# A four-layer cross-attention and FFN kernel on one core: router rows normalised tile by tile, first queries tile by tile, layer 1's conversions a gap earlier

## The chip, the cores and the metric

The kernel runs on one core of one Trainium2 chip. The metric is device microseconds of one execution; before the change the median of three executions is 1113.09 us (1112.28 to 1113.81). Engines are named as the profile names them: PE multiplies and transposes, DVE does vector work, ACT does activations and scaled copies, POOL does small vector work here and issues the indirect DMAs (gathers and scatters), SP issues the plain DMAs. Each engine runs its own instructions in the order in which they stand in its program; waits between engines are semaphores.

## What is computed

The input x is 2048 rows (tokens) of 256 values, in 8 batches of 256 rows. Four layers follow each other, and each adds a cross-attention over 77 context rows and then an FFN to x, both read from a normalised copy of x:

```python
x = x + jnp.tanh(g_xattn[1]) * _L1_xattn_ref(_layernorm(x), ctx, ctx, ...)   # one head
x = x + jnp.tanh(g_ffn[1])   * _L1_ffn_ref(_layernorm(x), W1, b1, W2, b2)    # rows quantised to 8 bits, ternary weights, 256 -> 1024 -> 256
x = x + jnp.tanh(g_xattn[2]) * _L2_xattn_ref(_layernorm(x), ctx, ctx, mask, 64, ...)  # 16 heads, the best 64 of 77 scores kept
x = x + jnp.tanh(g_ffn[2])   * _L2_ffn_ref(_layernorm(x), router_w, w1, w2)  # 8 experts, each row goes to its best 2, capacity 640
```

In layer 2's FFN the logits are `x_flat @ router_w.T` of the normalised rows; a row's place in its expert's buffer is a running count over all rows before it. Layers 0 and 3 are of the same build and are not touched.

## The kernel before

**Groups and tiles.** x stays on the chip in four groups `X[0]` to `X[3]` of 512 rows, each of `GT` = 4 tiles of 128 rows. Layer 0 is done for all groups first (to about 224 us of the span). Layer 1 is `cross1(g)` (attention of a group) and `ffns1(g)` (FFN of a group). Group 0 passes through both, and group 1 through `cross1`, before anything of layer 2 starts; the other groups are worked on between the tiles of layer 2.

**Layer 2's selection** is `select(n0, n1)` (L1398), a loop over the 16 tiles, run in two halves, tiles 0 to 7 and 8 to 15. `distances` makes a tile's scores (`sc`, L1052) from the queries of its group; ACT turns them into distances from the maximum (`pr`, L1072); then DVE drops the 13 lowest of 77 scores for 16 heads, with 2 x 16 MAX8 (L1410) and 2 x 16 MATCH_REPLACE8 (L1422). After every eighth of these it calls `gap()` (L1383): eight gaps a tile. In a gap the generators in `steps` are advanced, each in every second gap: `finish(n)` of the tiles before, `route`, `places`, `queries`, and `front`, which is layer 1's groups 1 to 3 (`groups1`). DVE's order is written out in this way by hand (`manual_schedule` with DVE alone); the order on PE, ACT, POOL and SP is chosen when the program is built, by a scheduler that goes by program order, by priority (`high_priority(AHEAD)`) and by when it takes an instruction to be ready.

**Queries.** `queries(g)` normalises a whole group (`normal_act`: bn_stats and bn_aggr on DVE, four small POOL operations, four ACT `xn` at L245, eight PE transposes L255, two ACT copies) and multiplies (`pq`, L1031, four matmuls of 128x512). `queries(0)` stands ahead of `select`, so tile 0 of the selection waits for all of group 0.

**End of a tile.** `finish(n)` (L1078): Abs and Exp on ACT (L1083, L1084), sums on DVE (`sm`, L1088), a product on POOL (L1090), transposes `pta` (L1096), copies `aT`, `po` (L1102), `oT2`, `py` (L1110, L1112), and, six of its steps after the start, the DVE operation at L1115 that adds the tile's result to x. At the last tile of a group it appends `route(g)`.

**Router.** `route(g)` (L1121) normalises the whole group with `normal_act`, writes it to DRAM (`xbuf`, one DMA of 512 KB for each half that needs it, six in all), three steps later multiplies 4 x 2 times with the router's weights (`pl`, L1141), a step later starts the softmax (`m`, L1148, `pb`, L1151) and a step later takes the best two experts. After groups 1 and 3 follows `places(h)`: it counts, by matmuls with triangular and block matrices (`ptc`, `pcn`, `pp`), each row's place, finds which expert each 128-row tile belongs to (`widx`), and inverts the places by 16 matmuls (`inv`, L1351, with `at_row`, L1348) into the rows of each tile (`tok`, L1364, `gate`, `row`).

**Experts.** `experts(h)` (L912) fetches a tile's rows from `xbuf` (`xg`, L919, needs `tok`) and its expert's weights of 2 MB (`wt`, L924, needs `widx`), transposes the rows (`ptm`), multiplies (`phm`, L948, then GELU `hT` L952, `pym`, L960), scales (`yo`, L965) and scatters into `ybuf` (L970). `experts(0)` has 16 tiles and runs beside the second half of the selection; `experts(1)` needs `places(1)`, has 22 and more, and runs beside layer 3.

**Layer 1's FFN.** `ffn1(n)` is one tile: quantised rows `xi`, transposes `ptx` (L664), `ph` (L672, L676) with GELU (`h`, L677); two steps later the row maximum `am2` (L681) and an ACT pass that scales and rounds (L686); at the next step `hi` (L688, DVE, to bf16), eight transposes `pth` (L691), a copy `hiT` (L693), `pyf` (L696); at the next step the add to x (L700). `ffns1` starts the tiles in pairs and advances a tile at every second call.

**PSUM.** Eight banks. Ahead of the selection a pool of eight is split into five for `cross1(0)` and `ffns1(0)` and three for the rest; it is closed, and then three (`psm`), two (`psc`, the scores) and three (`ps`) are opened.

Of the kernel before, what the change touches and what calls it, by code (L numbers as in the profile page):

```python
# [9 lines left out]
F32 = mybir.dt.float32  # L10
# [9 lines left out]
P = 128  # L20
D = 256
# [37 lines left out]
def flamingo_kernel(ctx: ExitStack, tc: tile.TileContext, io: dict):  # L59
# [597 lines left out]
    def ffn1(n, ps, f1w, xn, up, dn, rT):  # L657
# [29 lines left out]
        yield  # L687
# [11 lines left out]
        yield  # L699
        nc.vector.scalar_tensor_tensor(  # L700
# [3 lines left out]
    def ffns1(g, ps, f1w, act):  # L704

        for rows in normal1(g, ps, f1w, act):
            yield
            yield
        fs = {}
        at = 0  # L710
        while at == 0 or fs:
            if at % 4 < 2 and (n := at // 4 * 2 + at % 2) < GT:
                fs[n] = ffn1(g * GT + n, ps, f1w, *rows)
            for n in [n for n in fs if n % 2 == at % 2]:
                if next(fs[n], fs) is fs:
                    del fs[n]
            at += 1
            yield
# [90 lines left out]
    with tc.tile_pool(name="a1p", bufs=8, space=PSUM, side="right", reuse_waits="tile") as ps:  # L809
        chain, ps = Banks(ps, "chain", 5), Banks(ps, "beside", 3)  # L810
        for _ in cross1(0, chain, b1w, *kv1, False):
            pass
        for _ in ffns1(0, chain, b1w, False):
            pass
        for _ in cross1(1, ps, b1w, *kv1, False):
            pass

        nm = a2.tile([P, NB, SK], BF16, name="nm")
        nmf = nm.rearrange("p b k -> p (b k)")
        nc.vector.tensor_copy(nmf, mask_u8)
        some = a2.tile([P, NB], F32, name="some")
        nc.vector.tensor_reduce(some, nm, AX.X, ALU.max)
        nc.vector.tensor_scalar(nmf, nmf, 2.0**100, -(2.0**100), ALU.mult, ALU.add)
        onesb = a2.tile([P, P], BF16, name="onesb")
        nc.vector.memset(onesb, 1.0)
        bq4 = a2.tile([P, KC], F32, name="bq4")  # L830
        nc.vector.tensor_scalar(bq4, cols[:, C_WQB * KC : (C_WQB + 1) * KC], 0.25, None, ALU.mult)
        wob3 = rows3(a2, V_WOB, "wob")

        kT2 = a2.tile([P, KC, NB, 2, SK], F32, name="kT2")
        V2 = a2.tile([SK, NB, 8, 2, 2, 16], F32, name="V2")
        nc.gpsimd.memset(V2.rearrange("p b r q s d -> p (b r q s d)"), 0.0)

        for hb in range(2):  # L840
            for oc in range(KC):
                pk = ps.tile([P, 512], F32, name="pk", tag="ps")
                for kc in range(KC):
                    nc.tensor.matmul(
                        pk[:, :HB], wk2[:, kc, oc * P : (oc + 1) * P],
                        ctxT[:, kc, hb * HB : (hb + 1) * HB],
                        start=(kc == 0), stop=(kc == KC - 1),
                    )
                for q in range(2):
                    nc.vector.tensor_scalar(  # L850
                        kT2[:, oc, 4 * hb : 4 * hb + 4, q, :],
                        pk[:, :HB].rearrange("p (b k) -> p b k", k=SK),
                        col(C_WKB, oc), par[:, q : q + 1], ALU.add, ALU.mult,
                    )
            for b in range(4 * hb, 4 * hb + 4):
                pv = ps.tile([P, 512], F32, name="pv", tag="ps")
                for kc in range(KC):
                    nc.tensor.matmul(
                        pv[:SK, :D], ctxT[:, kc, b * SK : (b + 1) * SK], wv2[:, kc, :],
                        start=(kc == 0), stop=(kc == KC - 1),  # L860
                    )
                pvv = pv[:SK, :D].rearrange("p (r q d) -> p r q d", q=2, d=16)
                bvv = vrow(V_WVB, SK).rearrange("p (r q d) -> p r q d", q=2, d=16)
                for q in range(2):
                    nc.vector.tensor_add(V2[:, b, :, q, q, :], pvv[:, :, q, :], bvv[:, :, q, :])

# [45 lines left out]
    def experts(h, psm, f2w, widx, tok, gate, row, ahead=0):  # L912
# [91 lines left out]
    psm = ctx.enter_context(tc.tile_pool(name="f2p", bufs=3, space=PSUM, reuse_waits="tile"))  # L1004
    banks = ExitStack()
    psc = banks.enter_context(
        tc.tile_pool(name="a2s", bufs=1, space=PSUM, side="right", reuse_waits="tile")
    )
    ps = banks.enter_context(
        tc.tile_pool(name="a2p", bufs=3, space=PSUM, side="right", reuse_waits="tile")  # L1010
    )
# [11 lines left out]
    qs = {}  # L1023

# [53 lines left out]
    def finish(n, pr):  # L1078
# [28 lines left out]
        oT = a2w.tile([P, KC, P], F32, name="oT2")  # L1107
# [9 lines left out]
        )  # L1117
        if t == GT - 1:
            steps.append(route(g))

    def route(g):  # L1121

        gs = slice(g * GT, (g + 1) * GT)

# [3 lines left out]
        bank = ps if g else psm  # L1128
        xn, xT = normal_act(g, bank)
        for h in range(g // 2, 2):  # L1130
            r = g % 2 * GN + (h - g // 2) * HN
            nc.sync.dma_start(
                out=xbuf[h][r : r + GN, :].rearrange("(t p) d -> p t d", p=P), in_=xn
            )
        yield
        yield
        yield
        pl = bank.tile([P, GT, NE], F32, name="pl", tag="ps")
        for t in range(GT):
            for kc in range(KC):  # L1140
                nc.tensor.matmul(  # L1141
                    pl[:, t, :], xT[:, kc, t * P : (t + 1) * P], rtr[:, kc, :],
                    start=(kc == 0), stop=(kc == KC - 1),
                )
        yield
# [252 lines left out]
    def select(n0, n1):  # L1398
# [4 lines left out]
        for n in range(n0, n1):  # L1403
            pr = nxt
            ahead = distances(n + 1) if n + 1 < n1 else iter(())
            rows = [pr[:, j, c, :] for j in range(4) for c in range(4)]
            for r in range(2):
                m8 = a2w.tile([P, H, 8], F32, name=f"m8{r}")
                for i, row in enumerate(rows):
                    nc.vector.max(m8[:, i, :], row)  # L1410
                    if i == H - 1:
                        while n + 1 < n1 and (n + 1) // GT not in qs:
                            gap()
                        with tc.high_priority(AHEAD):
                            nxt = next(ahead, None)
                    if i % 8 == 7:
                        gap()
                if r == 1:

                    nc.vector.memset(m8[:, :, NDROP - 8 :], -BIG)  # L1420
                for i, row in enumerate(rows):
                    nc.vector.match_replace(row, m8[:, i, :], row, -BIG)  # L1422
                    if i % 8 == 7:
                        gap()
# [7 lines left out]
    ordered = {mybir.EngineType.DVE}  # L1432
    with tc.manual_schedule(engines=ordered):
        with tc.high_priority(AHEAD):
            for _ in queries(0):
                pass
        front = groups1(psm, kv1)
        steps.append(front)
        select(0, HT)
        last = steps.pop()  # L1440
        while steps:
            gap()
# [327 lines left out]
```

## Time and profile before

| what | value |
|---|---|
| median of three executions | 1113.09 us |
| the profiled execution | 1113.11 us |
| its span, first to last instruction | 1111.3 us |
| PE busy | 911.4 us (82%) |
| DVE busy | 645.9 us (58%) |
| ACT busy | 511.2 us (46%) |
| POOL busy | 307.6 us (28%) |

Times below are microseconds from the start of the span. In the timeline the selection's first MAX8 stands at 302.8, tile 7's add to x at 541.9, the first expert matmul at 597.3, the selection's last MATCH_REPLACE8 at 729.1, the add of tile 15 at 758.1, and the first matmul of `experts(1)` at 805.1. A busy share is an average over stages with different limits, so the stages between these marks are read one by one.

### The profile page before, as it was taken

Reading aid. Unit: us, or ns where it says so; the run is one execution under the profiler, and the core shown is the slowest. Engines: PE = TensorE matmul, PEld = TensorE weight load, DVE = VectorE, ACT = ScalarE, POOL = GpSimd, SP = SyncE. Lnnn points to the kernel's source line nnn. Section 1 sums busy time; section 2 is a strip of 40 time slices with the busy share of each in tenths; the row PEclk is TensorE's granted clock in tenths of the full one; section 3 lists DMA queues with packets and bytes.
Section 4 is the critical chain, followed back from the end, with each engine's and each line's share of the span. In section 5 each row is a group of like instructions: output and inputs, shape, how many; then the busy total and the mean of one; then the engine's idle time right before and its main releaser. Section 6 shows DMA issues by size and latency. Waiting matters only on the chain.

```text
span 1111.3 us, 16751 instructions
## 1 busy us (share of the span) xinstructions
PE 911.4 (82%) x5896; PEld 667.3 (60%) x5896; DVE 645.9 (58%) x2834; ACT 511.2 (46%) x1026; POOL 307.6 (28%) x333
## 2 busy tenths in 40 slices
PE   4678798848968688696877998899999969897895
PEld 2456565634525344463455776787999867696663
DVE  4767966656586976988676687732700023501663
ACT  3333444117356576575555566644222236422551
POOL 2342124010020210120104233243345445331531
PEclk9668989978965776865566999999999989998696
DMA  6200000003000000010106544365888964383001
GB/s 227 94 1 3 1 1 1 1 1 152 1 1 1 1 1 1 1 39 1 39 1 229 193 168 175 116 230 201 301 307 319 360 237 180 105 300 124 10 10 38
DMA packets 27179, 115.77 MB, mean 104 GB/s; under 512 B 4324, under 2 KB 16332, under 8 KB 21973
## 3 DMA queue, kind: packets, MB, share of 16 engines
q0 software_dynamic: 9504, 90.71, 22.3%
q1 hardware_dynamic: 17589, 23.96, 6.0%
q8 instruction: 48, 0.79, 0.3%
q14 instruction: 38, 0.31, 0.1%
HBM read 99.19 MB, written 15.47 MB: 103 GB/s over the span
## 4 chain that ended last, share of the span: by engine, by line
PE 40%; DVE 25%; ACT 12%; POOL 9%; issue 8%; DMA 6%; SPq 1%; POOLq 0%; ACTq 0%; DVEq 0%
DVE pr L1422 3%; PE phm L948 3%; PE pta L1096 3%; DVE m L1410 3%; PE pym L960 3%; DMA yg<-ybuf 3%; PE py L488 2%; DMA ybuf<-yo,row 2%; PE po L1102 2%; PE pta L473 2%; POOL pr L1090 2%; DVE sm L1088 2%; PE ph L672 2%; ACT pr L1072 1%; POOL ybuf L970 1%
## 5 line engine op out<-in xcount | busy, mean ns | idle before, releaser
L948 PE MATMUL phm<-xgT,wt 128*128 128x128 f32 x1216 | 152.5, 280 | 1.4 <-DMA wt<-in_w,widx 0.9
L948 PEld LDWEIGHTS phm<-xgT,wt 128*128 128x128 f32 x1216 | 147.0, 195 | 5.7 <-issue 2.6
L960 PE MATMUL pym<-wt,hT 128*128 128x256 f32 x608 | 146.2, 385 | 3.0 <-ACT hT L952 3.0
L960 PEld LDWEIGHTS pym<-wt,hT 128*128 128x128 f32 x608 | 112.1, 193 | 18.5 <-ACT hT L952 4.4
L1422 DVE MATCH_REPLACE8 pr<-m,pr 128x77 f32<-128x77 f32 x512 | 107.3, 224 | 0.0
L1090 POOL TENSOR_TENSOR pr<-pr,sm 128x1232 f32<-128x1232 f32 x16 | 36.0, 2249 | 179.9 <-DVE sm L1089 161.6
L952 ACT ACTIVATE hT<-phm 128x512 f32<-128x512 f32 x76 | 45.4, 597 | 81.1 <-PE phm L948 81.0
L1410 DVE MAX8 m<-pr 128x8 f32<-128x77 f32 x512 | 76.2, 222 | 0.0
L1096 PE MATMUL pta<-ident,pr 128*77 128x128 f32 x256 | 54.2, 352 | 18.4 <-POOL pr L1090 18.3
L1570 DVE TENSOR_TENSOR x<-x,yg 128x512 f32<-128x512 f32 x16 | 12.9, 808 | 94.7 <-DMA yg<-ybuf 94.7
L970 POOL DMA_INDIRECT ybuf<-yo,row x46 | 45.9, 997 | 74.0 <-ACT yo L965 58.3
L1098 ACT COPY aT<-pta 77x512 f32<-77x512 f32 x64 | 36.5, 588 | 61.8 <-PE pta L1096 61.8
L919 POOL DMA_INDIRECT xg<-xbuf,tok x38 | 38.6, 1015 | 93.9 <-PE ptm L935 42.2
L474 ACT COPY aT<-pta 77x512 f32<-77x512 f32 x64 | 35.4, 581 | 62.1 <-PE pta L473 62.1
L1072 ACT ACTIVATE pr<-sc,mx 128x77 f32<-128x77 f32 x256 | 58.8, 337 | 7.7 <-DVE mx L1067 7.7
L1052 PE MATMUL sc<-kT,qT 32*128 32x154 f32 x256 | 39.5, 406 | 26.9 <-ACT pr L1072 22.1
L456 POOL TENSOR_TENSOR pr<-pr,sm 128x1232 f32<-128x1232 f32 x16 | 36.8, 2299 | 89.1 <-DVE sm L455 45.6
L965 ACT ACTIVATE yo<-pym,gate 128x256 f32<-128x256 f32 x38 | 18.1, 476 | 93.4 <-PE pym L960 47.5
L924 POOL DMA_INDIRECT wt<-in_w,widx x38 | 37.2, 979 | 79.7 <-PE pym L960 71.0
L1096 PEld LDWEIGHTS pta<-ident,pr 128*77 128x77 f32 x256 | 37.8, 190 | 33.0 <-POOL pr L1090 21.3
L473 PE MATMUL pta<-ident,pr 128*77 128x128 f32 x256 | 44.7, 319 | 15.4 <-POOL pr L456 9.6
L473 PEld LDWEIGHTS pta<-ident,pr 128*77 128x77 f32 x256 | 33.4, 170 | 31.1 <-issue 12.9
(388 smaller groups left out, 1947.2 us busy)
## 6 DMA issues: line engine op xcount, KB each, us to landing
ybuf<-zero SPq DMA_DIRECT2D x8, 512.0 KB, 4.7
yg<-ybuf SPq DMA_DIRECT2D x16, 256.0 KB, 8.9
xbuf<-xn SPq DMA_DIRECT2D x6, 512.0 KB, 2.8
x<-in_x SPq DMA_DIRECT2D x4, 512.0 KB, 5.0
raw_f1w<-in_f1w SPq DMA_DIRECT2D x2, 1024.0 KB, 4.8
out<-x SPq DMA_DIRECT2D x8, 256.0 KB, 2.1
vec<-in_vec SPq DMA_DIRECT2D x1, 896.0 KB, 9.9
ybuf<-yo,row POOLq DMA_INDIRECT x46, 6.0
```

The costliest lines, as they stand in the source:

```text
L473: nc.tensor.transpose(pt[:SK, j, :], pn2[i][:, j, c, :], ident)
L919: nc.gpsimd.indirect_dma_start(out=xg[:, :], out_offset=None, in_=xbuf[h][:, :], in_offset=bass.IndirectOffsetOnAxis(ap=tok[:, m : m + 1], ...
L948: nc.tensor.matmul(ph[:, i, :], wt[:, kc * FF + fc * P : kc * FF + (fc + 1) * P], xgT[:, kc, :], start=(kc == 0), stop=(kc == KC - 1),)
L952: nc.scalar.activation(hT[:, NFC // 2 * fq : NFC // 2 * (fq + 1), :], ph, AF.Gelu)
L960: nc.tensor.matmul(py, hT[:, fc, :], wt[:, KC * FF + fc * D : KC * FF + (fc + 1) * D], start=(fc == 0), stop=(fc == NFC - 1),)
L970: nc.gpsimd.indirect_dma_start(out=dst[:, :], out_offset=bass.IndirectOffsetOnAxis(ap=row[:, m : m + 1], axis=0), in_=yo[:, :], in_offset= ...
L1052: nc.tensor.matmul(sc[:, jj, c * 2 * SK : (c + 1) * 2 * SK], qT[32 * j : 32 * j + 32, c, t * P : (t + 1) * P], kT2[32 * j : 32 * j + 32, c ...
L1072: nc.scalar.activation(pr[:, j0 + jj, c, :], sc[:, jj, c * SK : (c + 1) * SK], AF.Identity, bias=mx[:, jj, c : c + 1], scale=-1.0,)
L1090: nc.gpsimd.tensor_tensor(pr, pr, sm.unsqueeze(3).to_broadcast([P, 4, 4, SK]), ALU.mult)
L1096: nc.tensor.transpose(pt[:SK, j, :], pr[:, j, 2 * c + q, :], ident)
L1410: nc.vector.max(m8[:, i, :], row)
L1422: nc.vector.match_replace(row, m8[:, i, :], row, -BIG)
```

## The change

`route` no longer normalises a group. A new helper `normal_tile` does one tile, right behind the tile's add to x in `finish`; the tile's rows go to `xbuf` at once (128 KB each, 24 DMAs in place of six) and two steps later to the router's matmul, whose result is copied to an SBUF tile `logits`. At the last tile of a group `finish` goes straight on into `route`, which starts at the softmax. `queries(0)` is replaced by `queries0(t)`, one call for each tile of group 0: tile 0 ahead of the selection, tile 1 at its start, tiles 2 and 3 within tiles 0 and 1. Layer 2's keys (`pk`) are computed ahead of `cross1(1)`, its values (`pv`) behind it. The PSUM pools of the selection are opened ahead of layer 1's group 0, which now has three banks in place of five. In `ffns1` a tile whose ACT pass has just been issued is advanced at the next call and not at the one after it. The buffers of `oT2` (two, of 1 KB a partition) are shared with the new `xn_q0` and `xT_q0`.

```diff
@@ ffn1 @@
         nc.scalar.activation(h, h, AF.Identity, bias=magic, scale=up2)
-        yield
+        yield "soon"
         nc.vector.tensor_scalar(hi, h, MAGIC, 127.0, ALU.subtract, ALU.min)
...
         yield
+        yield
         nc.vector.scalar_tensor_tensor(
             X[g][:, t, :], py[:, :D], dn2, X[g][:, t, :], ALU.mult, ALU.add
         )
@@ ffns1 @@
         fs = {}
+        soon = set()
...
-            for n in [n for n in fs if n % 2 == at % 2]:
-                if next(fs[n], fs) is fs:
+            for n in [n for n in fs if n % 2 == at % 2 or n in soon]:
+                soon.discard(n)
+                step = next(fs[n], fs)
+                if step is fs:
                     del fs[n]
+                elif step:
+                    soon.add(n)
@@ layer 1's group 0 @@
-    with tc.tile_pool(name="a1p", bufs=8, space=PSUM, side="right", reuse_waits="tile") as ps:
-        chain, ps = Banks(ps, "chain", 5), Banks(ps, "beside", 3)
-        for _ in cross1(0, chain, b1w, *kv1, False):
-            pass
-        for _ in ffns1(0, chain, b1w, False):
-            pass
-        for _ in cross1(1, ps, b1w, *kv1, False):
-            pass
+    psm = ctx.enter_context(tc.tile_pool(name="f2p", bufs=3, space=PSUM, reuse_waits="tile"))
+    banks = ExitStack()
+    psc = banks.enter_context(
+        tc.tile_pool(name="a2s", bufs=1, space=PSUM, side="right", reuse_waits="tile")
+    )
+    ps = banks.enter_context(
+        tc.tile_pool(name="a2p", bufs=3, space=PSUM, side="right", reuse_waits="tile")
+    )
+    for _ in cross1(0, psm, b1w, *kv1, False):
+        pass
+    for _ in ffns1(0, psm, b1w, False):
+        pass
...
-        for hb in range(2):
-            for oc in range(KC):
-                pk = ...
-            for b in range(4 * hb, 4 * hb + 4):
-                pv = ...
+    for hb in range(2):
+        for oc in range(KC):
+            pk = ...
+    for _ in cross1(1, ps, b1w, *kv1, False):
+        pass
+    for b in range(NB):
+        pv = ...
@@ new helpers @@
+    def normal_tile(x, bank):
+        xn = a2w.tile([P, D], F32, name="xn_q0", tag="oT2")
+        xT = a2w.tile([P, KC, P], F32, name="xT_q0", tag="oT2")
...
+        nc.vector.bn_stats(st, x)
+        nc.vector.bn_aggr(mv, st)
+        rs = small.tile([P, 1], F32, name="q0_rs")
+        nc.gpsimd.tensor_scalar(rs, mv[:, 1:2], EPS, None, ALU.add)
+        nc.gpsimd.tensor_tensor(rs, rs, mhalf[:, :1], ALU.pow)
+        m = small.tile([P, 1], F32, name="q0_nm")
+        nc.gpsimd.tensor_tensor(m, mv[:, 0:1], rs, ALU.mult)
+        nc.gpsimd.tensor_scalar(m, m, -1.0, None, ALU.mult)
+        nc.scalar.activation(xn, x, AF.Identity, bias=m, scale=rs)
+        pt = bank()
+        for kc in range(KC):
+            nc.tensor.transpose(
+                pt[:, kc * P : (kc + 1) * P], xn[:, kc * P : (kc + 1) * P], ident
+            )
+        nc.scalar.copy(xT, pt.rearrange("p (c n) -> p c n", c=KC))
+        return xn, xT
+
+    def queries0(t):
...
+            _, xT = normal_tile(
+                X[0][:, t, :], lambda: ps.tile([P, KC * P], F32, name="ptq0", tag="ps")
+            )
+            pq = ps.tile([P, KC * P], F32, name="pqq0", tag="ps")
+        for oc in range(KC):
+            for kc in range(KC):
+                nc.tensor.matmul(
+                    pq[:, oc * P : (oc + 1) * P], wq2[:, kc, oc * P : (oc + 1) * P],
+                    xT[:, kc, :], start=(kc == 0), stop=(kc == KC - 1),
+                )
+            nc.scalar.activation(
+                qs[0][:, oc, rows], pq[:, oc * P : (oc + 1) * P], AF.Identity,
+                bias=bq4[:, oc : oc + 1], scale=0.25,
+            )
@@ finish @@
-        oT = a2w.tile([P, KC, P], F32, name="oT2")
+        oT = a2w.tile([P, KC, P], F32, name="oT2", tag="oT2")
...
+        xn, xT = normal_tile(X[g][:, t, :], lambda: ps.tile([P, KC * P], F32, name="ptr", tag="ps"))
+        for h in range(g // 2, 2):
+            r = g % 2 * GN + (h - g // 2) * HN + t * P
+            nc.sync.dma_start(out=xbuf[h][r : r + P, :], in_=xn)
+        yield
+        yield
+        if t == 0:
+            logits[g] = f2.tile([P, GT, NE], F32, name="logits", bufs=2)
+        pl = ps.tile([P, NE], F32, name="pl", tag="ps")
+        for kc in range(KC):
+            nc.tensor.matmul(
+                pl, xT[:, kc, :], rtr[:, kc, :], start=(kc == 0), stop=(kc == KC - 1)
+            )
+        nc.vector.tensor_copy(logits[g][:, t, :], pl)
         if t == GT - 1:
-            steps.append(route(g))
+            yield from route(g)
@@ route @@
+        pl = logits.pop(g)
-        bank = ps if g else psm
-        xn, xT = normal_act(g, bank)
-        for h in range(g // 2, 2):
-            r = g % 2 * GN + (h - g // 2) * HN
-            nc.sync.dma_start(
-                out=xbuf[h][r : r + GN, :].rearrange("(t p) d -> p t d", p=P), in_=xn
-            )
-        yield
-        yield
-        yield
-        pl = bank.tile([P, GT, NE], F32, name="pl", tag="ps")
-        for t in range(GT):
-            for kc in range(KC):
-                nc.tensor.matmul(
-                    pl[:, t, :], xT[:, kc, t * P : (t + 1) * P], rtr[:, kc, :],
-                    start=(kc == 0), stop=(kc == KC - 1),
-                )
-        yield
@@ select @@
+            if n == 0:
+                with tc.high_priority(AHEAD):
+                    queries0(1)
...
                     nc.vector.max(m8[:, i, :], row)
+                    if r == 1 and i == 0 and n + 2 < GT:
+                        with tc.high_priority(AHEAD):
+                            queries0(n + 2)
@@ ahead of the selection @@
+    with tc.high_priority(AHEAD):
+        queries0(0)
     with tc.manual_schedule(engines=ordered):
-        with tc.high_priority(AHEAD):
-            for _ in queries(0):
-                pass
```

## The prediction

> **What bounds the kernel now.** First the busy time of each engine in the stages between the marks of the table (windows view; busy us, instructions, granted PE clock, DMA share).
>
> ```profile
> core 0: us, PE busy (x) PEld busy (x) DVE busy (x) ACT busy (x) POOL busy (x), PEclk, DMA share, GB/s
> 240.00:303.00 63.00, 49.70 (x256) 29.05 (x256) 39.64 (x129) 27.90 (x47) 7.78 (x10) 0.86 0.17 67
> 303.00:525.00 222.00, 168.96 (x926) 96.45 (x925) 181.24 (x1048) 136.88 (x293) 36.46 (x42) 0.66 0.02 6
> 525.00:597.00 72.00, 52.77 (x272) 32.27 (x273) 55.20 (x334) 36.35 (x72) 9.32 (x10) 0.57 0.13 46
> 597.00:805.00 208.00, 190.84 (x1451) 160.97 (x1449) 122.34 (x769) 113.86 (x235) 71.29 (x69) 0.96 0.57 203
> ```
>
> Up to 303 PE sets the pace: its timeline is almost without gaps from 249 to 303, and DVE waits for it. From 303 to 597 DVE leads (181 of 222, 55 of 72), and what it loses are waits. From 597 to 805 PE leads: 191 of 208, its gaps of 0.5 us and more between 600 and 770 sum to about 15. From 805 on the order of the instructions does not change, so a shift at 805 is a shift of the end.
>
> Next what DVE waits for in 303 to 600 (line, releaser: total us, times, longest), then the two waits ahead of the selection and the one ahead of the router's softmax (timeline: start, us, instruction, idle before and releaser).
>
> ```profile
> DVE x L700 <- PE pyf L696: 16.6, 4, 9.7
> DVE am L681 <- ACT h L677: 6.7, 3, 4.2
> DVE m L1148 <- PE pl L1141: 5.0, 1, 5.0
> ```
>
> ```profile
> 297.85 0.80 DVE L1067 TENSOR_REDUCE mx<-sc 128x8 f32<-128x616 f32 x1 [7.06 <-PE sc L1060]
> 302.06 0.80 DVE L1067 TENSOR_REDUCE mx<-sc 128x8 f32<-128x616 f32 x1 [3.41 <-PE sc L1060]
> 554.10 0.19 DVE L1148 TENSOR_REDUCE m<-pl 128x4 f32<-128x32 f32 x1 [4.99 <-PE pl L1141]
> ```
>
> Last, the entrance to the experts: `tok` is written at 584.4 to 584.8, then POOL issues two gathers, and PE multiplies at 597.26.
>
> ```profile
> 585.09 1.23 POOL L919 DMA_INDIRECT xg<-xbuf,tok  x1 [39.99 <-PE pth L691]
> 586.62 0.96 POOL L924 DMA_INDIRECT wt<-in_w,widx  x1 [0.30 <-issue]
> ```
>
> Issue to landing is 4.7 us for xg and 9.4 for wt (medians), so the weights, issued second and needing only `widx` (ready some 9 us earlier), end the wait.
>
> **The change, part by part.** The sum is made against the profiled execution, 1113.11 us (span 1111.3 and 1.8 around it), which stands at the median, 1113.09.
>
> 1. *Start of the selection.* Ahead of the second MAX8 PE now does keys of layer 1's group 1 (4.5 us) and all of queries(0): transposes 0.6 + 0.6, matmuls 2.7 + 1.1, 5.1 in all. The keys stand elsewhere and two tiles' queries remain (2.6), which saves 7.0. Against it: `pk` (2 x 2.24) moves ahead of cross1(1), where only part of it is covered by gaps, cost about 1.7; three banks in place of five in layer 1's group 0, estimated 1. I take -4. Bounds: -8 (all saved, more overlap) and 0 (the banks eat it; `ffns1(0)` is 30 us of interleaved tiles, one wait of the size of the 4.2 us on L677 would do).
>
> 2. *First half of the selection.* "soon" puts `hi` and `pyf` a gap earlier and the add at L700 later, so its 16.6 us of waits should go. But in the new order `hi` follows the ACT pass directly: that pass (1.28) stands behind the distances (16 x .34, 1.82 left at that point), so DVE waits some 3 to 5 us in group 1 and about 1 in groups 2 and 3. Of 16.6 I keep 10 as waits of the new kind: -6.6; behind `hi` stand the MAX8 of the tile, so each of these waits is paid in full. The softmax's wait on `pl` falls from 5.0 to 1 (only one tile is left to multiply): -4. Added on DVE ahead of `tok`: 20 rows, 4.8 us by the rows they resemble (bn_stats .41, bn_aggr .18, copies .16 to .2): +5, paid, for DVE leads here. ACT gets four more table loads in this half at 1.28 each, 5.1 us, mostly in ACT's idle time (137 of 222 busy): +1.5. Sum -4. Bounds: -14 (all waits of L700 go and ACT hides its part) and +5 (they are only replaced).
>
> 3. *Weights ahead of rows.* In the new order both first weight gathers stand before `xg` and `tok` on POOL. Then `tok` to first matmul is xg alone: 0.3 + 1.2 + 4.7 + transposes, about 6.5 in place of 12.5: -6. Bounds -6 and 0 (if `widx` is late, or POOL's normalising rows, now queued around the gathers, hold them).
>
> 4. *Queries of groups 2 and 3 ahead of the experts.* 8 transposes and 4 matmuls (5.5 us), before at 610.9 behind the first expert matmuls, now stand ahead of them, in time in which PE waits: -5 (bounds -5.5 and 0).
>
> 5. *597 to 805, PE's stage.* In the new order the experts' tiles are further along: at tile 15's `py` 14.0 of 16 are done in place of 11.3, and all 16 stand ahead of the second `inv`. Work that covered the hand-over is so spent. From the end of the last `pl` (768.0) to the first possible matmul of experts(1) the chain is: counts and places on DVE to 793.3 (`xg` issued), 4.7 to landing, .5 of transposes: 30. PE has now only 17.4 us to do there (2.4 expert tiles at 7.25): idle 12.6, where today it is 0.46 (PE's timeline, idle before the first matmul of experts(1)):
>
> ```profile
> 804.21 0.42 PE L935 MATMUL ptm<-ident,xg 128*128 128x128 f32 x2
> 805.09 1.16 PE L948 MATMUL phm<-xgT,wt 128*128 128x128 f32 x8 [0.46 <-ACT xgT L937]
> ```
>
>    New stalls: after a tile's add the circle DVE (.6), POOL (four rows, 2.0 at 280.6), ACT (.5), PE, ACT (.4), PE, about 4.9 us with hops, and between `py` and `ptr` PE has 3.5, 12.5, 13.6, 13.6, 10.7, 16.7, 4.6 and 3.2 us of work: short of 4.9 at three tiles, about +3. Behind a waiting `ptr` the experts' matmuls are queued. The two waits at whole-group normalising (2.3 and 1.8 us gaps at 698.5 and 763.6, and others) fall away: -6. Sum +9.6, taken as +9. Bounds: -3 (hand-over covered) and +30 (rival a).
>
>    POOL's 60 more rows are 2.0 us a tile beside 71 of 208 busy, but its queue also issues `xg`, `wt` and `ybuf`, about 1 us each: `rs` may stand behind some of them, which is priced in rival a. SP gets 18 more DMAs (128 KB for 512 KB, 24 for 6); SP is idle there, a write of 512 KB lands in 2.8 us, and nothing waits for it but `xg` of the last tile: 0 (bounds 0 and 2.8 at each of two hand-overs).
>
> Sum: -4 -4 -6 -5 +9 = -10, with some rounding in favour: **1102 us** (1113.1 - 11).
>
> *A rule against this change.* The table load at L677 takes 1.28 us, and the next row begins as it ends:
>
> ```profile
> 327.24 0.38 ACT L1072 ACTIVATE pr<-sc,mx 128x77 f32<-128x77 f32 x1
> 327.63 1.28 ACT L677 ACT_TABLE_LOAD   x1
> 328.93 0.69 ACT L677 ACTIVATE h<-ph,q_dn 128x512 f32<-128x512 f32 x1
> ```
>
> The Trainium skill, "ScalarE: Activation LUTs", section "What ACT_TABLE_LOAD costs", adds a drain and puts a switch at about 2.66 us. The order has 43 loads for 37: 7.7 us of ACT by the row, 16 by the rule, which would turn the +1.5 into about 3 and the forecast into 1104. The trace shows no such drain as a gap, so I go by the row.
>
> **The rivals.**
>
> (a) *The experts run dry; slower.* Eight tiles of the second half each add a circle through DVE, POOL, ACT and PE into PE's queue. For it: POOL issues gathers of 1 us, DVE has in the new order 8 to 9 us of work between a tile's add and its logits copy, the row and its transpose share two buffers with the next tile's `oT2`, and today `x` already waits 63.3 us for `py` in this stage. If each tile stalls PE by 2 us (a POOL row behind two issues), that is 16, with the 12.6 of the hand-over 28.6; against it stand the 6 + 5 at the entrance, since the 4 of the start go into DVE's added 5: 1113 + 17 = 1130. It decides once the loss in this stage exceeds the 15 to 19 us won before it (steps 1 to 4, with or without step 2). Against it: PE has more than 10 us of other work between `py` and `ptr` at five of eight tiles.
>
> (b) *Waits are only replaced.* `hi` waits for ACT where the add waited for `pyf`, DVE's 5 us are paid, and the hand-over takes what the entrance gives: -4 + 5 - 11 + 12 = +2, within 1111 to 1115. The change "doing nothing" is this case too: if the ACT pass comes so late that `hi` a gap earlier buys nothing.
>
> (c) *More than forecast.* L700's waits all go (-14), and half of the hand-over is covered: -4 -14 -6 -5 +3 = -26: about 1087.
>
> **How the numbers follow.** 0.2% is 2.2 us, about what a measurement of this kernel can tell from no change. Forecast, 1094 to 1108: .42. Case (c), under 1094: .15. A small gain, to 1110.9: .06. Case (b): .10. Slower, case (a) and milder forms: .27. So faster .63, same .10, slower .27. The range runs from 1087 (c) to 1121 (half of a); outside I leave .06 below and .14 above. The forecast side alone would be 1087 to 1111.
>
> **What would show it.** First MAX8 some 4 us earlier than 302.8; L700's wait on `pyf` under 5 us in total and a new one of `hi` on L686 of 3 to 10; `m` on `pl` about 1; `tok` some 8 us earlier; 6 to 7 us from `tok` to the first `phm`, with `wt` issued before `xg`; a PE gap of about 12 us ahead of experts(1). Wrong if PE's waits for `ptr` or `pl` sum to over 10 us between 597 and 805, if the first half does not shorten, or if the gap at the hand-over is absent or twice as long.

## The result and the profile after

The changed kernel takes 1154.89 us (median of 5 executions, 1148.84 to 1157.73) where the kernel before takes 1113.09 (5 executions beside it, 1108.72 to 1113.81): 1.0368 times as long, 95% interval 1.0336 to 1.0399. The forecast was 1102 with a range to 1121, so it failed in sign and in size.

The profiled execution is the shortest of the five, 1148.84 us with a span of 1147.0. Cut into the same five stretches, the two spans compare as follows (us; the tiles are those of the selection):

| stretch | before | after | difference |
|---|---|---|---|
| start to the second tile's first MAX8 | 325.1 | 318.5 | -6.6 |
| to `tok` of the first half | 259.3 | 282.9 | +23.6 |
| `tok` to the first expert matmul | 12.9 | 12.8 | -0.1 |
| to the first matmul of experts(1) | 207.8 | 225.0 | +17.2 |
| to the end | 306.2 | 307.8 | +1.6 |
| span | 1111.3 | 1147.0 | +35.7 |

The windows view of the kernel after, on its own marks (columns as in the prediction):

```profile
318.50:601.40 282.90, 213.10 (x1159) 126.48 (x1158) 208.44 (x1193) 171.29 (x346) 46.32 (x72) 0.62 0.05 17
...
614.20:839.20 225.00, 194.84 (x1432) 166.10 (x1433) 120.02 (x755) 111.57 (x231) 75.10 (x87) 0.91 0.50 181
```

DVE is busy for 208.4 us of the first line and was busy for 203.3 between the same marks before. So 5.1 of the 23.6 us are its added work, and 18.5 are added idle time. What that idle time waits for, between the same marks of the kernel after:

```profile
DVE logits L1185 <- PE pl L1182: 31.8, 6, 13.5
DVE hi L688 <- ACT h L686: 8.6, 5, 4.9
DVE am L681 <- ACT h L677: 8.3, 3, 4.8
DVE x L701 <- PE pyf L696: 4.6, 2, 3.4
```

Between the same marks before, the longest row of DVE's waits was this one:

```profile
DVE x L700 <- PE pyf L696: 15.9, 3, 9.7
```

These 15.9 us on `pyf` are down to 4.6 (L701 after the change), and `hi`, which waited 1.2 us for ACT before, now waits 8.6. The first line of the view after is new: DVE's copies of the tiles' logits, 0.17 us of work each, make DVE stand for 31.8 us. In PE's stage, 614 to 839, the same line leads again:

```profile
DVE logits L1185 <- PE pl L1182: 65.9, 7, 13.6
DVE x L1168 <- PE py L1165: 16.1, 3, 12.3
DVE logits L1185 <- issue: 12.2, 1, 12.2
```

The stage before had these two at the top:

```profile
DVE x L1115 <- PE py L1112: 63.3, 7, 14.8
DVE m L1148 <- PE pl L1141: 7.9, 1, 7.9
```

So 71 us of waits on `py` and `pl` have become 94: 16.1 on `py`, and 78 at the logits (13.6 at the longest; for 12.2 of them the profile shows no releaser).

One tile shows how such a wait comes about. ACT's, PE's and DVE's timelines for tile 0's router row (start, us, engine and line, idle before and releaser):

```profile
376.29 0.37 ACT L1049 COPY xT_q<-ptr 128x256 f32<-128x256 f32 x1 [0.78 <-PE ptr L1046]
```

```profile
385.53 1.86 PE L255 MATMUL pt<-ident,xn 128*128 128x128 f32 x4
388.06 1.12 PE L255 MATMUL pt<-ident,xn 128*128 128x128 f32 x4 [0.68 <-ACT xT L258]
389.86 3.78 PE L1084 MATMUL pq<-xT,w_wq 128*128 128x512 f32 x4 [0.68 <-ACT xT L258]
393.43 0.42 PE L255 MATMUL pt<-ident,xn 128*128 128x128 f32 x1
393.64 2.58 PE L1084 MATMUL pq<-xT,w_wq 128*128 128x512 f32 x4
396.15 0.53 PE L1105 MATMUL sc<-kT,qT 32*128 32x154 f32 x4
396.52 0.23 PE L1113 MATMUL sc<-nm,onesb 1*128 1x154 bf16 x2
396.68 0.61 PE L1182 MATMUL pl<-w_rtr,xT_q 128*128 128x8 f32 x4
```

```profile
397.33 0.17 DVE L1185 COPY logits<-pl 128x8 f32<-128x8 f32 x1 [6.54 <-PE pl L1182]
399.08 2.33 DVE L1466 MAX8 m<-pr 128x8 f32<-128x77 f32 x16
```

The row is transposed and copied at 376.7. The four small matmuls that read it come 20 us later, since PE's order puts another tile's `pta` and `po` (377 to 385, not shown), transposes of other rows and the next group's queries ahead of them, with PE's own waits for ACT among those. DVE reaches the copy 6.5 us too soon, and behind it in DVE's order stand the next tile's MAX8. From `xT` to `pl` it is 20.0, 20.1, 7.0, 9.2, 5.7, 11.1, 1.5 and 0.1 us in tiles 0 to 7.

The entrance to the experts after the change (POOL, then PE, then ACT):

```profile
592.59 1.25 POOL L936 DMA_INDIRECT wt<-in_w,widx  x1 [0.81 <-ACT xn L245]
594.14 1.05 POOL L936 DMA_INDIRECT wt<-in_w,widx  x1 [0.30 <-issue]
602.10 0.95 POOL L931 DMA_INDIRECT xg<-xbuf,tok  x1 [6.91 <-DVE pad L1423]
```

```profile
607.70 0.27 PE L947 MATMUL ptm<-ident,xg 128*128 128x128 f32 x1
...
614.21 1.65 PE L960 MATMUL phm<-xgT,wt 128*128 128x128 f32 x6 [2.54 <-ACT xgT L949]
```

```profile
611.32 1.32 ACT L1136 ACTIVATE pr<-pr,some 128x1232 f32<-128x1232 f32 x1 [1.70 <-issue]
612.67 1.23 ACT L1137 ACTIVATE pr<-pr 128x1232 f32<-128x1232 f32 x1
613.80 0.35 ACT L949 COPY xgT<-ptm 128x256 f32<-128x256 f32 x1
```

The weights are fetched ahead of `tok`, and PE transposes the first rows 6.3 us after `tok` (601.4). But the second transpose and the copy `xgT` stand behind the distances of the next tile, and the copy behind Abs and Exp too, until 613.8.

Last the hand-over to experts(1), PE's timeline:

```profile
823.16 5.25 PE L1404 MATMUL inv<-of_tile,at_row 128*128 128x50 f32 x32 [3.25 <-DVE at_row L1401]
836.90 0.69 PE L947 MATMUL ptm<-ident,xg 128*128 128x128 f32 x2 [8.49 <-DMA xg<-xbuf,tok]
```

PE has run out of expert tiles and stands for 3.25 + 8.49 = 11.7 us.

### The profile page after: what moved, and what is told of

The parts are those of the page before. It is cut to its first block, busy times and chain, and to the rows that moved or that the text cites. A ratio compares the mean times of both kernels' runs of the same rounds, so it can differ in the third digit from the quotient of the medians.

```text
span 1147.0 us, 16947 instructions
## 1 busy us (share of the span) xinstructions
PE 922.5 (80%) x5920; PEld 680.3 (59%) x5920; DVE 651.5 (57%) x2850; ACT 523.4 (46%) x1048; POOL 325.8 (28%) x393
## 4 chain that ended last, share of the span: by engine, by line
PE 45%; DVE 23%; ACT 11%; POOL 7%; DMA 6%; issue 6%; SPq 0%; POOLq 0%; ACTq 0%; DVEq 0%
PE phm L960 6%; PE pym L972 4%; PE pta L1149 4%; DVE pr L1481 3%; DMA yg<-ybuf 3%; DMA ybuf<-yo,row 2%; PE pta L473 2%; PE po L1155 2%; DVE m L1466 2%; PE py L488 2%; PE pyf L696 2%; PE ph L672 1%; POOL pr L1143 1%; PE po L476 1%; PE sc L1105 1%
## 5 line engine op out<-in xcount | busy, mean ns | idle before, releaser
L960 PE MATMUL phm<-xgT,wt 128*128 128x128 f32 x1216 | 157.9, 287 | 5.0 <-ACT xgT L949 2.5
L960 PEld LDWEIGHTS phm<-xgT,wt 128*128 128x128 f32 x1216 | 152.6, 202 | 10.2 <-ACT yo L977 3.3
L1628 DVE TENSOR_TENSOR x<-x,yg 128x512 f32<-128x512 f32 x16 | 12.9, 813 | 95.6 <-DMA yg<-ybuf 89.6
L1185 DVE COPY logits<-pl 128x8 f32<-128x8 f32 x16 | 2.6, 165 | 109.9 <-PE pl L1182 97.6
L1038 POOL TENSOR_SCALAR q_rs<-q_mv 128x1 f32<-128x1 f32 x20 | 5.0, 248 | 191.1 <-DVE q_mv L1036 190.7
L473 PEld LDWEIGHTS pta<-ident,pr 128*77 128x77 f32 x256 | 33.3, 170 | 31.4 <-issue 12.8
## 6 DMA issues: line engine op xcount, KB each, us to landing
yg<-ybuf SPq DMA_DIRECT2D x16, 256.0 KB, 12.6
```

What stands on the lines that cost most here:

```text
L473: nc.tensor.transpose(pt[:SK, j, :], pn2[i][:, j, c, :], ident)
L960: nc.tensor.matmul(ph[:, i, :], wt[:, kc * FF + fc * P : kc * FF + (fc + 1) * P], xgT[:, kc, :], start=(kc == 0), stop=(kc == KC - 1),)
```

## The experiments

Three explanations were set against each other. **Theory A**: DVE, whose order is fixed by hand, stands before `pl`, and that is the loss. **Rival B**: the loss is the new order and load on PE and ACT, whatever DVE does (the hand-over idle, the copy `xgT`). **Rival C**: the loss comes from the start or from `hi` waiting for ACT. Each experiment is an edit of the kernel before or after; ratios are to the kernel before on the same chip, with 95% intervals. Waits and stretches are read from one traced execution of each kernel, which can lie 8 us off the median (wait away: 1105.06 for 1112.97; start alone: 1113.92 for 1107.83).

### The parts one by one

Three parts can be taken alone: the *start* (`queries0`, keys, pools), *soon* (the conversion in the next gap) and the *router* (`normal_tile`, a `pl` and a copy per tile).

**Router taken back** (the start and soon remain).

```diff
-        xn, xT = normal_tile(X[g][:, t, :], lambda: ps.tile([P, KC * P], F32, name="ptr", tag="ps"))
...
-            yield from route(g)
+            steps.append(route(g))
```

> The changed kernel with the router's normalising taken back to whole groups (finish and route as before); queries tile by tile, keys, PSUM pools and the conversion in the next gap stay. Theory A (DVE's copies of the logits wait for pl, which PE reaches 4 to 20 us after its input is ready; 31.8 us of DVE idle before tok and 66 behind it): the loss goes, 1098 to 1112 us. Rival B (the loss is the new order of the experts on PE and the idle hand-over, whatever DVE does): the router's part is also what moved them, so 1100 to 1120. Rival C (the loss comes from the start or from hi waiting for ACT): stays at 1140 or above.

Measured: 1111.93 us, ratio 0.9977 (0.9937 to 1.0016). The loss is gone, so it needs the router's part; C in its plain form falls. A and B both allow this. The start's gain (below) shows here in part at most.

**Router alone**, in the kernel before.

> The kernel before with the router's part alone (normal_tile behind each tile's add, 128 KB writes, pl and a logits copy per tile). Theory A: 1140 to 1160 us, DVE waits of over 25 us on pl before tok. Rival B: 1125 to 1160, with an idle hand-over of PE of about 12 us. Rival C: 1105 to 1118.

Measured: 1135.21 us, ratio 1.0171 (1.0080 to 1.0262). DVE waits 26.4 us on `pl` ahead of `tok`, and a hand-over idle of 3.25 + 7.78 = 11.0 us is there as well. This is under A's range and within B's; C falls as a cause by itself. And 22 us (by the interval 9 to 29) is about half of the loss.

**Start alone.**

> The kernel before with the start alone: queries of group 0 tile by tile, layer 2's keys ahead of cross1(1), PSUM pools opened early. Router and layer 1's conversions as before. If the start is worth what its first tiles show (the second tile's first MAX8 at 319 in place of 325): 1104 to 1110 us. If the earlier start is lost again in waits further on: 1111 to 1115. If three banks in place of five cost more than they bring: above 1115.

Measured: 1107.83 us, ratio 0.9937 (0.9914 to 0.9960). A gain of 7 us by the ratio, as the first expectation has it, and the lowest median of all versions. Which stretch holds the gain is not shown: in the traced execution, the slowest of nine, the second tile's first MAX8 comes at 317.7 for 325.1, but `tok` at 584.6 for 584.4.

**Soon alone.**

```diff
-        yield
+        yield "soon"
         nc.vector.tensor_scalar(hi, h, MAGIC, 127.0, ALU.subtract, ALU.min)
```

> The kernel before with layer 1's conversion a gap earlier, alone. From e_late_no_soon (7 us faster than e_copy_late) I expect a loss: 1115 to 1121 us, with waits of hi for ACT of 6 to 10 us. If the conversion only loses beside the router's tiles: 1107 to 1114.

Measured: 1112.33 us, ratio 0.9982 (0.9961 to 1.0003): no difference that can be told, so the expected loss did not come. Waits of `hi` for ACT are 7.7 us, and waits on `pyf` fall from 15.9 to 8.4: one was put in the place of the other.

**Start and router without soon** (the edit above taken back in the changed kernel).

> The changed kernel with the conversion back at its old place (start and router stay). If hi's waits for ACT add to the waits for pl: 1140 to 1150 us. If the two waits cover each other: 1151 to 1158.

Measured: 1132.86 us, ratio 1.0153 (1.0113 to 1.0194), 22 us under the changed kernel, less than both expectations. A part worth nothing alone makes half of the loss beside the router.

**Router and soon without the start.**

> The kernel before with the router's part and the earlier conversion, without the start. If the earlier conversion collides with the router's tiles: 1148 to 1160 us (1135 of the router alone and some 20). If it takes all three parts: 1130 to 1140.

Measured: 1146.28 us, ratio 1.0300 (1.0270 to 1.0330): 11 us more than the router alone, between the two expectations. Soon costs time beside the router's tiles with or without the start, and with it more.

### The place of the copy and of `pl`

**Copy by ACT in place of DVE.**

```diff
-        nc.vector.tensor_copy(logits[g][:, t, :], pl)
+        nc.scalar.copy(logits[g][:, t, :], pl)
```

> The changed kernel with the logits copied by ACT in place of DVE; everything else as it is. Theory A: DVE no longer waits for pl, about 20 us come back before tok and some behind it, 1115 to 1135 us (ACT now waits for pl, which takes part of the gain). Rival B: PE's order is as before, the hand-over stays, 1145 to 1158. Rival C: 1145 to 1158.

Measured: 1138.76 us, ratio 1.0221 (1.0136 to 1.0307), 16 us back of 42, a little short of A's range. DVE's waits on `pl` are gone, but the softmax now waits 8.1 us for ACT's copy ahead of `tok`. The hand-over idle is 13.2 us.

**Copy by DVE, later.** The edit adds two steps of `finish`, which is four gaps and not two as the expectation has it.

```diff
+        yield
+        yield
         nc.vector.tensor_copy(logits[g][:, t, :], pl)
```

> The changed kernel with DVE's logits copy two gaps (one step of finish) later, pl where it was in the program. Theory A: most of the waits of 4 to 13 us on pl are covered by MAX8 and MATCH_REPLACE8 of the next tile, 1115 to 1138 us. Rival B: 1145 to 1158. Rival C: 1145 to 1158. Against all: pl holds one of three PSUM banks two gaps longer, and the softmax of a group is two gaps later, which could cost 2 to 5 us.

Measured: 1122.99 us, ratio 1.0081 (1.0047 to 1.0115). Of the 42 us 32 are back, as A has it. `pl` comes 20.0 and 18.2 us after `xT` in tiles 0 and 1, as late as in the changed kernel; only DVE is elsewhere meanwhile. Its wait on `pl` ahead of `tok` is 8.0 in place of 31.8, and the hand-over idle of PE falls from 11.7 to 3.1, although no instruction of that place was touched. So the idle hand-over, which B counts as a cause, follows from the waits at least in part. Ahead of `tok`, though, only 9 us come back (273.9 for 282.9), since waits on `py` rise from 1.5 to 10.3 and others with them; 18 come back in PE's stage (207.1 for 225.0):

```profile
DVE logits L1187 <- PE pl L1182: 8.0, 2, 5.1
```

```profile
602.80:809.90 207.10, 184.52 (x1448) 155.17 (x1449) 128.86 (x811) 117.26 (x243) 76.93 (x89) 0.99 0.54 190
```

**The same without start and soon** (router alone, copy later).

> The kernel before with the router tile by tile and DVE's logits copy two steps (four gaps) later; no start, no earlier conversion. Theory A (the copy's place on DVE is most of the router's cost of 22 us): 1116 to 1124. If most of the cost is the per-tile normalising itself (POOL, ACT, PE order): 1127 to 1136.

Measured: 1116.43 us, ratio 1.0010 (0.9987 to 1.0034), in A's range: of the router's 22 us all but a few are the copy's place. The router decides on the right numbers here, and all that was edited against the router alone is the two steps ahead of DVE's copy.

**The same without soon** (start, router, copy later).

> e_copy_late with layer 1's conversions back at their old place (no 'soon'). If the conversion a gap earlier is worth its price (pyf waits gone against new waits of hi for ACT): 2 to 8 us slower than e_copy_late, 1125 to 1131. If hi's new waits for ACT (8 to 10 us) cost as much as they save: within 3 us of 1123. If they cost more: 1112 to 1120.

Measured: 1116.17 us, ratio 1.0016 (0.9986 to 1.0047). Soon costs 7 us here, the third expectation. Without it 6.2 us of waits on `pl` ahead of `tok` are left, and with it 8.0.

**`pl` at high priority** for the scheduler, with DVE's order as it was.

```diff
+        with tc.high_priority(AHEAD):
             pl = ps.tile([P, NE], F32, name="pl", tag="ps")
...
             nc.vector.tensor_copy(logits[g][:, t, :], pl)
```

> The changed kernel with the router's matmul (pl) and its copy raised to the scheduler's high priority; DVE's order is the same. Theory A (DVE's copy waits because PE comes to pl late): PE does pl 5 to 15 us sooner after its transposes, DVE's waits on pl fall from 31.8 us before tok to under 18, time 1128 to 1145 us. Rival B (only the place of the copy in DVE's order matters, PE cannot do pl sooner because its own queue is busy): waits stay within 20 per cent of 31.8, 1148 to 1158.

Measured: 1149.7 us, ratio 1.0306 (1.0261 to 1.0351). The priority hardly moves `pl`: 19.4 us after `xT` in tile 0 in place of 20.0, and DVE's waits are 29.5. Both numbers are those of B as it is put here (PE's own queue keeps `pl` back). The edit didn't make the difference it was to test, so it says nothing for or against DVE's standing as the cause of the loss.

**Both** (priority, and copy later).

> Both remedies: pl at high priority and DVE's copy two steps of finish (four gaps) later. Theory A: DVE waits on pl under 5 us before tok, hand-over gap of PE under 3 us, 1112 to 1122 us, not above e_copy_late (1123) by more than 3. Rival B: the same as e_copy_late within 3 us.

Measured: 1126.23 us, ratio 1.0103 (1.0068 to 1.0139), as `pl` at its old priority within the intervals. A's forecast failed here in all its terms (wait ahead of `tok` 8.0, hand-over 3.1, time above 1122): the priority adds nothing.

**`pl` and copy earlier** by one step, two gaps.

> The changed kernel with pl and the copy one step of finish (two gaps) EARLIER in the program. Theory A, the dose from the other side: DVE stands longer in front of pl, waits before tok 40 to 70 us, 1165 to 1190 us. Rival B (PE's order decides, the copy's place on DVE does not): 1145 to 1160.

Measured: 1146.29 us, ratio 1.0300 (1.0258 to 1.0341), in B's range, where A as it stood expected 1165 or more. The wait on `pl` ahead of `tok` is 31.8 us again. The trace tells why: PE's order moved along, `pl` comes 8.3 and 11.9 us after `xT` in tiles 0 and 1 in place of 20.0 and 20.1. The place of the copy can't be changed alone in this direction, and the hand-over idle is 1.7 us here with 33 us of loss still there. So that idle is not what makes the loss: here it stands ahead of `tok` and at the entrance (287.1 and 16.2 us for 259.3 and 12.9 before).

### The wait taken away alone

What the copy reads is put in the place of where it stands: 8 columns of x, long ready. `pl` is multiplied as before and read by nobody.

```diff
-        nc.vector.tensor_copy(logits[g][:, t, :], pl)
+        nc.vector.tensor_copy(logits[g][:, t, :], X[g][:, t, :NE])
```

> The changed kernel, but DVE's logits copy reads 8 columns of x (long ready) and not pl; pl is still multiplied and read by nobody, so the router decides on other numbers and the output is not the reference's. Theory A (the loss is DVE standing before pl): at least 30 of the 42 us go, 1112 to 1126 us, tok 20 us or more earlier after the second tile's first MAX8. Rival B (the loss is the order and the load of PE and ACT, the wait on pl only covers other waits that come out in its place): 1135 to 1155.

Measured: 1112.97 us, ratio 1.0011 (0.9981 to 1.0041). With normalising, transposes, `pl`, copies and writes per tile all there, and the router deciding on other numbers, the time is that of the kernel before: in sum the 42 us are gone. DVE's waits of this kernel from the second tile's first MAX8 to `tok`, and its windows from there:

```profile
DVE am L681 <- ACT h L677: 10.8, 5, 4.2
DVE x L1168 <- PE py L1165: 8.6, 3, 3.9
DVE hi L688 <- ACT h L686: 8.2, 4, 3.8
```

```profile
313.30:586.00 272.70, 207.67 (x1143) 123.87 (x1147) 206.46 (x1170) 169.07 (x341) 44.08 (x67) 0.64 0.05 16
586.00:592.30 6.30, 0.69 (x2) 0.29 (x2) 6.27 (x48) 0.37 (x1) 4.61 (x7) 0.50 0.15 43
592.30:801.50 209.20, 190.75 (x1464) 160.14 (x1464) 129.85 (x819) 117.47 (x248) 79.04 (x90) 0.97 0.56 198
```

No line of `logits` is left among the waits, while `hi`'s wait for ACT is as long as in the changed kernel. The first stretch lasts 272.7 us for 282.9, the entrance 6.3 for 12.8, PE's stage 209.2 for 225.0, and PE stands 0.46 us at the hand-over. PE still multiplies `pl` 20.1 and 21.2 us after `xT` in tiles 0 and 1: being late costs nothing there when nobody stands before it. One expectation of A failed: `tok` comes 10.3 us earlier after the second tile's first MAX8, not 20 or more. Other waits have come in the place of most of the 31.8 (on `py` 8.6 for 1.5, on `sc` 6.8 for 0, for `pr` 6.6 for 2.0), and to this extent B was right that the wait covers others.

**The same without soon.**

> The same on e_no_soon (start and router, conversions at their old place); the output is again not the reference's. Theory A: e_no_soon's 1133 falls to 1108 to 1118 us, and the difference to e_x_logits shows what the earlier conversion costs without DVE's waits for pl: under 8 us if it is the two waits in series that made 22. Rival: the difference stays at 15 to 25, so the earlier conversion collides with something else of the router's tiles (ACT or PE).

Measured: 1112.18 us, ratio 0.9995 (0.9971 to 1.0019), the same as with soon. So soon costs nothing here without DVE's waits for `pl`.

**What this pair leaves open.** The five stretches of some traced executions (us):

| kernel | to the second tile | to `tok` | to the first expert matmul | to experts(1) | to the end |
|---|---|---|---|---|---|
| before | 325.1 | 259.3 | 12.9 | 207.8 | 306.2 |
| changed | 318.5 | 282.9 | 12.8 | 225.0 | 307.8 |
| start alone | 317.7 | 267.0 | 13.0 | 208.4 | 306.1 |
| router alone | 322.5 | 269.4 | 10.4 | 221.1 | 308.8 |
| router alone, copy later | 319.8 | 265.9 | 10.5 | 207.8 | 310.0 |
| changed, without soon | 320.3 | 270.6 | 10.4 | 221.0 | 308.9 |
| wait away | 313.3 | 272.7 | 6.3 | 209.2 | 301.7 |
| wait away, without soon | 320.7 | 270.2 | 19.3 | 201.8 | 298.2 |

No copy of the logits stands in the last stretch. In all kernels with the right numbers it takes 306.1 to 312.4 us, in the two with the wait away 301.7 and 298.2. So 6 to 11 us of what this pair gains lie where no such wait can be; that the router's other numbers make them is likely and not shown. The pair also takes away the waits of 5.0 and 7.9 us on `pl` that the kernel before had itself. It can't tell, then, whether some of the loss is the router's other work.

What carries A is the copy's place, with the right numbers: between router alone and router alone with the copy later 18 us go in the traces, 13 of them in PE's stage and 3.5 ahead of `tok`. A is shown as the cause of most of the loss; B falls as the main cause, and can stand only for the rest. With the copy later and without soon, the start's 7 us still do not show (1.0016 for 0.9937).

## Why the prediction was wrong, step by step

- **The step that failed is step 2**, "The softmax's wait on `pl` falls from 5.0 to 1 (only one tile is left to multiply)", and with it step 5, which has no term for such a wait. It weighed the one wait that the trace of before showed and moved it, and gave no price to the 16 new ones: every tile's copy is a DVE instruction that needs PE, at a fixed place in DVE's order. Measured, DVE's waits at the logits are 31.8 us ahead of `tok` and not 1, and 78 in PE's stage; moving the copy alone gave 32 of the 42 us back. Step 2's stretch came out at +23.6 for -4. Not all of that is the wait: with the start alone it is 7.7 us longer already. In the same stretch the prediction's other terms held: waits on `pyf` under 5 (4.6), `hi` 3 to 10 (8.6), DVE's added work 5 (5.1). The upper bound of +5 had no term for the new wait at all.
- **The comparison that hid it** stands in rival (a): 8 to 9 us of DVE's work between a tile's add and its copy, against a circle of 4.9 us. That circle counted the instructions of one row on bare engines. The row's way leads through queues: in tile 0, 20 us of PE's queue stood between `xT` and `pl`. Rival (a) had the right sign, but let PE wait for the rows, where DVE waits for PE.
- **Step 1** (-4): the start alone is worth 7 us (0.9937). The second tile's first MAX8 came 6.6 us earlier in the changed kernel. The first tile's came 22 us earlier (280.7 for 302.8), most of which is given back within tile 0. The bounds held at this mark; at `tok` the traced execution of the start alone has nothing left of it.
- **Step 3** (-6): measured 0 (12.8 for 12.9). Fetching the weights ahead of `tok` worked, and PE had the rows 6.3 us after `tok`. What the step left out is that the copy `xgT` stands in ACT's queue behind the distances, Abs and Exp. Where that queue was empty, the entrance was as forecast: 6.4 us with the copy by ACT, 6.3 with the wait away. With the wait away and without soon it was 19.3, with the queries of the next groups between `tok` and the first expert matmul.
- **Steps 4 and 5** (-5 and +9, together +4): measured +17.2. The hand-over idle was forecast at 12.6 and is 11.7 (its chain began at the end of the last `pl`, 768.9 in the trace and not 768.0, which moves it by less than 1); PE's other gaps of 0.6 us and more are 17.7 for 14.7, the +3 forecast. But the reason given for the hand-over, a fixed order of PE, was too simple: it goes (0.46) when only DVE's wait goes. The 5.5 us of queries that left the stage can't be seen, since PE is busy for 194.8 us in place of 190.6: the granted clock is 0.91 for 0.96 and a matmul `phm` takes 287 ns for 280 (means of the whole execution). With the same queries moved and the router by groups (router taken back), PE is busy for 184.4 at a clock of 0.97. That the lower clock follows from the waits is argued, not shown.
- **The table loads**: the prediction weighed the row's 1.28 us against the 2.66 of the Trainium skill ("ScalarE: Activation LUTs", section "What ACT_TABLE_LOAD costs"), and the trace after agrees with the row. There are 43 loads for 37 (55.2 us for 47.5), 1283 ns each, and the next instruction of ACT follows after a median of 11 ns; no drain is to be seen as a gap. Where a load falls does count: `hi`'s longest wait, 4.9 us, covers the end of a load (1.28), an Exp (1.23), eight distances (1.82) and the pass itself (1.28).
- **The small writes** (24 of 128 KB) land in 1.7 us for 2.8 (medians of the few landings that the traces show), and no row of the waits names them, as forecast.

What stays open is why soon, which costs nothing without DVE's waits on `pl`, costs 11 us (without the start) to 22 us (with it) beside them. From the second tile to `tok` the changed kernel's waits sum to 68.7 us, without soon to 55.0: `pyf` gives back 10.3, but `hi` takes 8.6, `pl` 4.8 more, `am` 3.2 more, and smaller ones 7.4 together (the longest, on `pyv`, 3.2). So read, the waits stand one behind the other and do not cover each other, but no run tests this. Why DVE waits longer for `pl` then is not settled either.

## What to carry to other kernels

An instruction that is put into a hand-ordered in-order queue and reads another engine's result is priced by when that engine's queue will reach the result, not by the length of the chain that feeds it. List every such new reader, find in the producer's order what stands between its input and its output with that work's own waits, and give the wait an upper bound even where the trace of before has no row for it. To test such a wait, move the reader alone; or let it read something that is ready and leave everything else, which tells a cause from its consequences (here the idle hand-over). Where that changes the numbers that later work depends on, compare also a stretch that the edit can't reach: here it moved by 6 to 11 us.

## What the runs showed that was not expected

- With DVE's waits on one small matmul taken away, PE's idle time at the hand-over went from 11.7 to 0.46 us and the granted clock of PE's stage from 0.91 to 0.97, on the router's other numbers. With the copy only moved, and the right numbers, they went to 3.1 us and 0.99.
- Two edits that cost 22 us (router) and nothing (soon) alone cost 33 us together (1.0300), and nothing, with the start beside them, once the wait was gone (1.0011).
- Within one kernel the mean granted clock goes with the time: nine of the ten executions with the wait away reach from 1105.1 us at 0.848 to 1118.7 us at 0.830, so half a per cent is to be told only from several executions. From kernel to kernel it does not: the changed kernel ran at 0.812 to 0.822, without soon at 0.844 to 0.852, and the kernel before, 19 us faster than the latter, at 0.833 to 0.845 beside it.
